# Two query chunks per slice of x, K before the second block of x, halved first slice and last sum, and a new instruction order, in a cross-attention kernel

## The chip, the core and the metric

The kernel runs on one core of one Trainium2 chip. The metric is device time in microseconds (us), the median of several executions. The core has a matrix engine (PE), a vector engine (DVE), an activation engine (ACT), a general engine (POOL), a queue engine that mostly issues transfers (SP), and 16 DMA engines that all transfers share.

## The reference

Two batches of 2048 tokens with 640 channels attend to 154 context rows of 1024 channels: 77 text rows and 77 image rows, each with its own softmax, 20 heads of 32 channels. Everything is float32.

```python
q = split_heads(x @ Wq.T)                       # (2, 20, 2048, 32)
k, v       = text @ Wk.T,  text @ Wv.T          # context rows 0..76
k_ip, v_ip = ip @ Wk_ip.T, ip @ Wv_ip.T         # context rows 77..153
out = softmax(q k^T / sqrt(32)) v + softmax(q k_ip^T / sqrt(32)) v_ip
return merge_heads(out) @ Wo.T + bo + x
```

## The kernel before, in words

Channels lie on the partitions. A batch is cut into blocks of 512 tokens (`xs`, four tiles of 128 x 5 x 512); one channel chunk `c` holds four heads (128 channels), so there are 5 chunks in each of 2 batches, 10 in all, and each has two halves of 1024 tokens: 20 units `u` (`step_of`, L116). A unit of batch 0 has its queries from two blocks of x, `(u, 0)` and `(u, 1)`; unit 0 is chunk 0 of blocks 0 and 1, unit 1 is chunk 0 of blocks 2 and 3, unit 2 is chunk 1 of blocks 0 and 1, unit 4 is chunk 2 of blocks 0 and 1.

Nothing is scheduled automatically. The order of the program is a list of some 900 words, `SCHEDULE` (L560), which `emit` (L630) turns into instructions one after the other; each engine carries out its own in that order. The letters that matter here:

- `q.u.h@bank`: the queries of a unit from one block, 5 matmuls of 128x512 (`queries`, L196-199; weights in `wqs`, three tiles used in turn); `cq.u.h`: ACT scales them into a tile `qT` (L207-209).
- `k.c.t`, `v.c.t`: the key or value projection of chunk `c`, for text or image rows, 8 matmuls (L136-140), with weights that `LK.n` loads (`load_w`, L126-130) into one of four slots; `ck`, `cv`: ACT copies the result (L684, L686).
- `R<s>.u@half`: the scores of a third of a unit, on a four-way row-tiled array into four of the eight PSUM banks (L224-231). `K`: ACT copies the four banks to `pb` (L239-243). `M`: DVE takes the row maxima (L275-282). `S`: POOL subtracts them (L291-293). `E`: ACT takes exponentials (L297-299, one instruction, or one per 77 scores with the maximum as its bias, L259-267, for the thirds in the sets `DIRECT` and `BIASED`; `DIRECT` reads the scores in PSUM and has no `K` and no `S`, `BIASED` has no `S`; `SUMMED` takes the row sums along). `D`, `I`, `N`, `T`: row sums and reciprocals on DVE, scaling on POOL (L312-314), a transpose on DVE (L318-321).
- `A.q@half`: probabilities times values for a chunk, 160 small matmuls into four banks (L323-330); `CA.q`: ACT empties those four banks (L347-357).
- `o`, `p`, `m`, `G`, `W`, `z`: the output projection of batch 0 by a fast scheme with 7 products, between the units of batch 1; `V`, `X`, `F`, `Y`: that of batch 1 by a longer scheme, in which `F` is one product (L839-846) and `Y` adds it to a sum on DVE (`add_part`, L786-796) and, with the last part, stores the sum from SP.
- `LX`, `LQ`, `LO`, `SF`, `SS`, `VS`: transfers, all issued from SP. Eight transfers may be under way; each waits for the one eight places earlier in its list.

The opening (L522-557) stands ahead of `SCHEDULE`. It issues block 0 of x in five slices and chunk 0 of Wq in five pieces, by turns from SP and ACT, then from SP block 1 of x, Wq chunk 1, half of the context, the first K weight, the other half, the second K weight, blocks 2 and 3 of x, and the V weights. PE makes 7 small matmuls on zeros, then three query chunks, `(0,0)`, `(0,1)` and `(2,0)`, each after the other, and then the two K projections of chunk 0. The first scores `R0.0` open `SCHEDULE`.

Of the kernel before, what the change touches and what calls it, by code (L numbers as in the profile page):

```python
# [9 lines left out]
F32 = mybir.dt.float32  # L10
# [4 lines left out]
B, S, C, CC, LT = 2, 2048, 640, 1024, 154  # L15
# [5 lines left out]
def kernel(  # L21
# [43 lines left out]
        (11, 0), (12, 0), (13, 0), (13, 2), (15, 1), (15, 2), (16, 2), (18, 1), (19, 2),  # L65
    }
    BIASED = {
        (3, 2), (4, 2), (6, 2), (8, 2), (9, 2), (11, 2), (12, 1), (14, 0), (18, 2),
    }
    SUMMED = {  # L70
        (4, 2), (11, 2), (12, 0), (13, 0), (13, 2), (14, 0), (15, 1), (15, 2), (18, 1), (18, 2), (19, 2),
# [3 lines left out]
    OPEN = 4  # L75
    HT = TB // 2

# [7 lines left out]
    wqs = [const.tile([P, NC, P], F32, name=f"wq_{n}") for n in range(3)]  # L85
# [5 lines left out]

    acc = const.tile([P, NC - 1, TB], F32, name="acc")
# [103 lines left out]
    def queries(u, h, pq):  # L196
        q = step_of(u)[0]
        for k in range(NC):
            nc.tensor.matmul(  # L199
                pq,  # L200
                wqs[q % 3][:, k, :],
                xs[place_of(u, h)][:, k, :],
                start=(k == 0),
                stop=(k == NC - 1),
            )

    def take_queries(u, h, pq):  # L207
        qT = qpool.tile([P, TB], F32, tag="qT", name=f"qT_{u}_{h}")
        nc.scalar.mul(qT, pq, SCALE)  # L209
        qTs[(u, h)] = qT  # L210
# [313 lines left out]
    for k in range(NC):  # L524
        load_x(queues[k % 2])
        queues[1 - k % 2].dma_start(out=wqs[0][:, k, :], in_=WqT[ts(k, P), :P])  # L526
    for _ in range(NC):
        load_x()
    load_wq(1)
# [11 lines left out]
    load_wq(2)  # L541
# [6 lines left out]
    FIRST = ((0, 0), (0, 1), (2, 0))  # L548
    for n, (u, h) in enumerate(FIRST):
        queries(u, h, banks[G + n])  # L550
        take_queries(u, h, banks[G + n])
    for t in range(2):
# [71 lines left out]
    ).split()  # L624

    late = [tuple(int(x) for x in w.split(".")[1:]) for w in SCHEDULE if w[:2] == "LX"]
    JOINS = {3: 5, 6: 1, 7: 6, 4: 7}
    at = {}

# [259 lines left out]
```

## Time and profile before

| what | us |
|---|---|
| median of 3 runs (lowest, highest) | 496.85 (496.82, 496.97) |
| the profiled execution, its own time | 497.84 |
| its span on the core | 496.0 |
| PE busy in the span | 489.1 |
| DVE busy | 413.0 |
| POOL busy | 370.3 |
| ACT busy | 301.4 |

Device time is a little more than the span, which runs from the first to the last record on the core. Views used later: a table by stage (busy time of each engine between two moments, with the number of instructions that start there, the mean granted TensorE clock, the share of the DMA engines and GB/s), the instructions in order of time (start, busy, engine, line, operation, tiles, shapes and count, and in brackets the idle time before with what ended it), and the chain that ended last, in order of time (start, length, what). A float32 matmul leaves two records, so `x10` is five matmuls. SPq and ACTq are the queues of SP and ACT at the issue of transfers; PEld is the load of weights.

### The profile page before, as it was taken

To read this page: it belongs to the slowest core of one execution; us is meant where nothing else is said; L and a number is where in the kernel's file an instruction comes from. 1 tells how busy PE (TensorE), PEld (TensorE's weight loads), DVE (VectorE), ACT (ScalarE), POOL (GpSimd) and SP (SyncE) were. 2 spreads that over 40 slices of the span, in tenths; PEclk is the share of its full clock that TensorE was granted. 3 is DMA by queue.
4 is the path that set the end of the run, shared out by engine and by line. 5 is a ranking of instruction groups with operands and counts; after the bars stand their busy time and mean duration, and the time that the engine had idled before them with its cause. 6 is when DMAs were issued, how large, how long until landed. Compare 5 with 4: busy or idle time off the path is not lost.

```text
span 496.0 us, 10378 instructions
## 1 busy us (share of the span) xinstructions
PE 489.1 (99%) x4114; PEld 288.5 (58%) x4114; DVE 413.0 (83%) x417; ACT 301.4 (61%) x929; POOL 370.3 (75%) x158
## 2 busy tenths in 40 slices
PE   8999999999999999999999999999999999999997
PEld 4676657467467556456556654754755675444442
DVE  0069999979999989979979796777999888999885
ACT  1175858977687778677999869677666962100000
POOL 0069998889988989788977798365989989249820
PEclk9999999999999999999999999999999999999999
DMA  8994404142425435395671359344551221510125
GB/s 267 351 260 128 120 3 130 49 112 74 109 65 170 125 120 165 119 380 204 194 236 49 113 159 316 133 127 140 166 174 45 62 91 42 171 63 23 43 85 211
DMA packets 67472, 69.38 MB, mean 140 GB/s; under 512 B 5472, under 2 KB 47200, under 8 KB 67424
## 3 DMA queue, kind: packets, MB, share of 16 engines
q1 hardware_dynamic: 66704, 68.00, 43.6%
q8 instruction: 32, 0.52, 0.5%
q10 hardware_dynamic: 720, 0.72, 0.5%
q14 instruction: 16, 0.13, 0.1%
HBM read 54.94 MB, written 10.49 MB: 132 GB/s over the span
## 4 chain that ended last, share of the span: by engine, by line
PE 95%; DMA 3%; SPq 1%; ACTq 0%; ACT 0%; DVE 0%; issue 0%
PE bank L199 33%; PE bank L846 11%; PE bank L330 11%; PE bank L231 11%; PE bank L488 10%; PE bank L140 9%; PE bank L469 7%; PE bank L498 3%; DMA aT<-in_L_xattn_Wk_ip_dram 2%; DMA x<-in_x_dram 1%; SPq L532 1%; ACTq L526 0%; SPq L130 0%; DVE acc L792 0%; ACT pb L243 0%
## 5 line engine op out<-in xcount | busy, mean ns | idle before, releaser
L314 POOL TENSOR_TENSOR pb<-pb,rden 128x1848 f32<-128x1848 f32 (+1 forms) x60 | 175.9, 2943 | 25.6 <-DVE rden L309 25.0
L199 PE MATMUL bank<-x,wq 128*128 128x512 f32 x400 | 179.6, 598 | 1.5 <-DMA x<-in_x_dram 1.4
L293 POOL TENSOR_TENSOR pb<-pb,mx 128x1848 f32<-128x1848 f32 (+1 forms) x42 | 128.2, 3066 | 58.5 <-DVE mx L279 58.3
L199 PEld LDWEIGHTS bank<-x,wq 128*128 128x128 f32 x400 | 73.5, 190 | 87.4 <-issue 81.6
L321 DVE STREAM_TRANSPOSE pb<-pb 128x1920 f32<-128x1920 f32 (+1 forms) x60 | 115.5, 1935 | 6.7 <-POOL pb L314 6.7
L279 DVE TENSOR_REDUCE mx<-pb 128x24 f32<-128x1848 f32 (+1 forms) x51 | 93.8, 1850 | 32.0 <-ACT pb L243 31.8
L243 ACT COPY pb<-bank 128x462 f32<-128x462 f32 (+1 forms) x204 | 87.1, 537 | 34.6 <-PE bank L231 34.0
L304 DVE TENSOR_REDUCE den<-pb 128x24 f32<-128x1848 f32 (+1 forms) x49 | 91.5, 1875 | 18.6 <-ACT pb L299 15.8
L299 ACT ACTIVATE pb<-pb 128x1848 f32<-128x1848 f32 (+1 forms) x42 | 69.3, 1651 | 18.6 <-POOL pb L293 18.5
L231 PEld LDWEIGHTS bank<-kT,qT 32*128 32x128 f32 x1280 | 45.5, 184 | 26.3 <-issue 16.6
L267 ACT ACTIVATE pb<-bank,mx 128x77 f32<-128x77 f32 x184 | 53.1, 380 | 10.8 <-DVE mx L282 10.8
L231 PE MATMUL bank<-kT,qT 32*128 32x154 f32 x1280 | 56.6, 306 | 0.3 <-ACT kT L557 0.3
L330 PE MATMUL bank<-pb,v 32*32 32x512 f32 x1600 | 55.2, 597 | 0.0
L267 ACT ACTIVATE pb<-pb,mx 128x77 f32<-128x77 f32 x160 | 47.3, 373 | 0.0
L140 PE MATMUL bank<-wo_ct,aT 128*128 128x154 f32 x320 | 45.8, 297 | 0.4 <-DMA aT<-in_L_xattn_Wk_ip_dram 0.4
L140 PEld LDWEIGHTS bank<-wo_ct,aT 128*128 128x128 f32 x320 | 42.8, 188 | 3.4 <-issue 2.2
L330 PEld LDWEIGHTS bank<-pb,v 32*32 32x32 f32 x1600 | 30.6, 103 | 21.6 <-issue 9.2
L209 ACT ACTIVATE qT<-bank 128x512 f32<-128x512 f32 x40 | 24.2, 614 | 27.4 <-PE bank L199 27.4
L267 ACT ACTIVATION_READ_ACCUMULATOR pb<-bank,mx 128x1 f32 x144 | 36.7, 258 | 0.0
L469 PE MATMUL bank<-aT,wo_ct 128*128 128x512 f32 x80 | 36.4, 595 | 0.0
L488 PE MATMUL bank<-aT,wo_ct 128*128 128x256 f32 x128 | 32.0, 384 | 0.0
L488 PEld LDWEIGHTS bank<-aT,wo_ct 128*128 128x128 f32 x128 | 23.8, 190 | 7.7 <-issue 4.5
(76 smaller groups left out, 427.9 us busy)
## 6 DMA issues: line engine op xcount, KB each, us to landing
x<-in_x_dram SPq DMA_DIRECT2D x20, 1280.0 KB, 7.3
out_dram<-acc SPq DMA_DIRECT2D x20, 256.0 KB, 2.6
x<-in_x_dram SPq DMA_DIRECT2D x18, 256.0 KB, 5.4
acc<-in_x_dram SPq DMA_DIRECT2D x16, 256.0 KB, 3.4
out_dram<-x SPq DMA_DIRECT2D x15, 256.0 KB, 2.0
v<-vS SPq DMA_DIRECT2D x160, 20.0 KB, 2.1
wq<-in_L_xattn_Wq_dram SPq DMA_DIRECT2D x9, 320.0 KB, 4.7
aT<-in_L_xattn_Wk_dram SPq DMA_DIRECT2D x5, 512.0 KB, 5.5
```

The costliest lines, as they stand in the source:

```text
L140: nc.tensor.matmul(keys_in(out), loaded[n][:, k, :], cT[:, k, :, t, :], start=(k == 0), stop=(k == NCC - 1))
L199: nc.tensor.matmul(pq, wqs[q % 3][:, k, :], xs[place_of(u, h)][:, k, :], start=(k == 0), stop=(k == NC - 1),)
L231: nc.tensor.matmul(ps[g][:, ts(t, 2 * L)], qTs[(u, h)][g * D : (g + 1) * D, ts(st, P)], kT[g * D : (g + 1) * D, c, b].rearrange("p t l -> ...
L243: nc.scalar.copy(keys_of(u, s)[:, :, g], ps[g][:, : n * 2 * L].rearrange("p (n l) -> p n l", n=n))
L267: nc.scalar.activation(row, row if ps is None else rows_in(ps[g], n)[:, t, x], AF.Exp, bias=maxs[(u, s)][:, *one], accum_out=None if den i ...
L279: nc.vector.tensor_reduce(mx, rows_of(u, s), AX.X, ALU.max, negate=negate)
L293: nc.gpsimd.tensor_tensor(rows_of(u, s), rows_of(u, s), maxs[(u, s)].unsqueeze(3).to_broadcast([P, n, 2, L]), ALU.subtract)
L304: nc.vector.tensor_reduce(den_of(u, s), rows_of(u, s), AX.X, ALU.add)
L314: nc.gpsimd.tensor_tensor(rows_of(u, s), rows_of(u, s), rdens[(u, s)].unsqueeze(3).to_broadcast([P, n, 2, L]), ALU.mult)
L321: nc.vector.transpose(p, p)
L330: nc.tensor.matmul(pa[r][g * D : (g + 1) * D, :], v4s[q % 2][rows, g, k, :], zones[rows, :, g, k, :], start=(k == 0), stop=(k == NK - 1),)
L488: nc.tensor.matmul(part, w_of[m][:, kp, op], t_of(m, b, i)[:, kp], start=(op == kp == 0 and m in (1, 2, 5)), stop=(op == 1 and kp == 1 and ...
```

## The change

- The opening gets chunks 0 and 1 of Wq together. Block 0 of x is loaded as before but its first slice comes in two halves of 256 tokens, from SP and ACT. PE makes chunks `(0,0)` and `(2,0)` side by side, both from each slice of x as it comes, the first slice in halves; then `(4,0)`, with Wq chunk 2, from the same block of x. `(0,1)` becomes the first word of `SCHEDULE`.
- SP's list after block 0: Wq chunk 2, context, first K weight, context, second K weight, then block 1 of x, block 2, the V weights, block 3.
- The queries `(2,0)` and `(4,0)` are kept in two tiles of `aT` that are free until chunk 3, not in `qpool`.
- The last `F` and the last `Y` of `SCHEDULE` are made in two halves of 256 columns, and the last sum is stored in two halves, one from SP and one from ACT.
- `DIRECT`, `BIASED` and `SUMMED` change for some thirds: in batch 0, `(3,2)` goes from biased to direct, and `(2,0)` and `(5,2)` become biased. In all ACT has 424 single-row exponentials in place of 344, 38 whole ones in place of 42, and 200 copies `K` in place of 204; POOL has 98 subtractions and scalings in place of 102.
- `SCHEDULE` is new from its first word to its last; the words are nearly the same.

```diff
     DIRECT = {
-        (11, 0), (12, 0), (13, 0), (13, 2), (15, 1), (15, 2), (16, 2), (18, 1), (19, 2),
+        (3, 2), (11, 0), (12, 0), (13, 0), (13, 2), (15, 0), (15, 1), (16, 2), (18, 1), (19, 2),
...
     BIASED = {
-        (3, 2), (4, 2), (6, 2), (8, 2), (9, 2), (11, 2), (12, 1), (14, 0), (18, 2),
+        (2, 0), (4, 2), (5, 2), (6, 2), (8, 2), (9, 2), (11, 2), (12, 1), (14, 1), (15, 2), (17, 2), (18,
+        2),
...
+    EARLY = (2, 0), (4, 0)
+    SIDES = slice(0, HT), slice(HT, TB)
...
+    q_early = aT[:, ds((NC - 1) * NHB, 2), :]
...
     queues = nc.sync, nc.scalar
-    for k in range(NC):
+    slices.pop(0)
+    for n, cols in enumerate(SIDES):
+        queues[n].dma_start(out=xs[0][:, 0, cols], in_=xT[:P, cols])
+        queues[1 - n].dma_start(out=wqs[n][:, 0, :], in_=WqT[:P, ts(n, P)])
+    for k in range(1, NC):
         load_x(queues[k % 2])
-        queues[1 - k % 2].dma_start(out=wqs[0][:, k, :], in_=WqT[ts(k, P), :P])
-    for _ in range(NC):
-        load_x()
-    load_wq(1)
+        queues[1 - k % 2].dma_start(
+            out=wq_all[:, :2, k, :], in_=WqT[ts(k, P), : 2 * P].rearrange("p (c o) -> p c o", c=2)
+        )
+    load_wq(2)
...
     load_w(2)
     load_w(3)
-    load_wq(2)
+    for _ in range(NC):
+        load_x()
...
-    FIRST = ((0, 0), (0, 1), (2, 0))
-    for n, (u, h) in enumerate(FIRST):
-        queries(u, h, banks[G + n])
-        take_queries(u, h, banks[G + n])
+    first = [(2 * c, 0, banks[G + c]) for c in range(3)]
+    for n, cols in enumerate(SIDES):
+        for c, (_, _, pq) in enumerate(first[:2]):
+            nc.tensor.matmul(
+                pq[:, cols], wqs[c][:, 0, :], xs[0][:, 0, cols], start=(n == 0), stop=False, skip_group_check=True
+            )
+    for k in range(1, NC):
+        for u, h, pq in first[:2]:
+            queries(u, h, pq, (k,), loose=True)
+    queries(*first[2])
+    for u, h, pq in first:
+        take_queries(u, h, pq)
...
     SCHEDULE = (
-        "R0.0@0 R1.0@1 K0.0 q.1.0@0 LK.5 SF.0.0 K1.0 M0.0 LK.4 M1.0 S0.0 R2.0@1 cq.1.0 v.0.0@1 K2.0 S1.0 M2.0 E0.0 "
...
-        "T1.1 S0.2 q.4.0@3 K1.2 T2.1 cq.3.1 S2.2 M1.2 E0.2 A.0@1 D0.2 S1.2 E2.2 cq.4.0 D2.2 I0.2 E1.2 N0.2 R0.3@0 "
-        "CA.0 D1.2 v.1.1@4 K0.3 I1.2 T0.2 N1.2 k.2.1@7 LK.11 cv.1.1 M0.3 R2.3@0 LK.13 ck.2.1 R1.3@1 LK.10 K2.3 T1.2 "
...
+        "q.0.1@4 R0.0@0 cq.0.1 LK.4 R1.0@1 K0.0 q.1.0@0 LK.5 K1.0 M0.0 M1.0 S0.0 R2.0@1 q.1.1@1 K2.0 S1.0 M2.0 E0.0 "
...
+        "cq.3.0 T2.0 R0.2@0 K2.2 k.2.1@5 I1.1 K0.2 I2.1 M2.2 N1.1 T0.1 R1.2@0 LK.8 LQ.3 v.1.0@6 K1.2 LK.13 M0.2 "
+        "N2.1 q.3.1@4 LK.10 T1.1 E0.2 S2.2 T2.1 M1.2 A.0@0 LQ.4 S1.2 cv.1.0 E2.2 D0.2 cq.3.1 ck.2.1 D2.2 E1.2 "
+        "R0.3@1 I0.2 I2.2 N0.2 CA.0 D1.2 v.1.1@0 K0.3 I1.2 N2.2 T0.2 cv.1.1 R1.3@1 R2.3@0 M0.3 N1.2 K1.3 k.2.0@4 "
...
-            nc.vector.tensor_tensor(t, t, ps, op)
+            for cols in sides:
+                nc.vector.tensor_tensor(t[:, cols], t[:, cols], ps[:, cols], op)
...
-            nc.sync.dma_start(out=outT[ts(m, P), ds(S + i * TB, TB)], in_=t)
+            for queue, cols in zip(queues, sides):
+                tokens = ds(S + i * TB + cols.start, cols.stop - cols.start)
+                queue.dma_start(out=outT[ts(m, P), tokens], in_=t[:, cols])
```

More of the change, by code (lines that the diff above doesn't have):

```diff
@@ L64 @@
     DIRECT = {
-        (11, 0), (12, 0), (13, 0), (13, 2), (15, 1), (15, 2), (16, 2), (18, 1), (19, 2),
+        (3, 2), (11, 0), (12, 0), (13, 0), (13, 2), (15, 0), (15, 1), (16, 2), (18, 1), (19, 2),
     }
     BIASED = {
-        (3, 2), (4, 2), (6, 2), (8, 2), (9, 2), (11, 2), (12, 1), (14, 0), (18, 2),
+        (2, 0), (4, 2), (5, 2), (6, 2), (8, 2), (9, 2), (11, 2), (12, 1), (14, 1), (15, 2), (17, 2), (18,
+        2),
     }
     SUMMED = {
-        (4, 2), (11, 2), (12, 0), (13, 0), (13, 2), (14, 0), (15, 1), (15, 2), (18, 1), (18, 2), (19, 2),
+        (3, 2), (4, 2), (11, 2), (12, 0), (13, 0), (13, 2), (14, 1), (15, 0), (15, 1), (17, 2), (18, 1),
+        (18, 2), (19, 2),
     }
@@ L74 @@
     NU = NP * SUB
-    OPEN = 4
+    EARLY = (2, 0), (4, 0)
     HT = TB // 2
+    SIDES = slice(0, HT), slice(HT, TB)
     const = ctx.enter_context(tc.tile_pool(name="const", bufs=1))
@@ L84 @@
     halves = banks[:G], banks[G:]
-    wqs = [const.tile([P, NC, P], F32, name=f"wq_{n}") for n in range(3)]
+    wq_all = const.tile([P, 3, NC, P], F32, name="wq_all")
+    wqs = [wq_all[:, n] for n in range(3)]
     bo_sb = const.tile([P, NC], F32, name="bo_sb")
@@ L194, with queries @@
     qTs = {}
-    def queries(u, h, pq):
+    def queries(u, h, pq, ks=range(NC), loose=False):
         q = step_of(u)[0]
-        for k in range(NC):
+        for k in ks:
             nc.tensor.matmul(
@@ L204, in queries @@
                 stop=(k == NC - 1),
+                skip_group_check=loose,
             )
     def take_queries(u, h, pq):
-        qT = qpool.tile([P, TB], F32, tag="qT", name=f"qT_{u}_{h}")
+        if (u, h) in EARLY:
+            qT = q_early[:, EARLY.index((u, h))]
+        else:
+            qT = qpool.tile([P, TB], F32, tag="qT", name=f"qT_{u}_{h}")
         nc.scalar.mul(qT, pq, SCALE)
@@ L523 @@
     queues = nc.sync, nc.scalar
-    for k in range(NC):
+    slices.pop(0)
[3 more added lines that the diff above has]
+    for k in range(1, NC):
         load_x(queues[k % 2])
-        queues[1 - k % 2].dma_start(out=wqs[0][:, k, :], in_=WqT[ts(k, P), :P])
-    for _ in range(NC):
-        load_x()
-    load_wq(1)
+        queues[1 - k % 2].dma_start(
+            out=wq_all[:, :2, k, :], in_=WqT[ts(k, P), : 2 * P].rearrange("p (c o) -> p c o", c=2)
+        )
+    load_wq(2)
     half = NCC // 2
@@ L560 @@
     SCHEDULE = (
[63 rows of a table removed]
[63 rows of a table added]
     ).split()
+    CLOSING = {[w for w in SCHEDULE if w[0] == kind][-1].partition("@")[0] for kind in "FY"}
     late = [tuple(int(x) for x in w.split(".")[1:]) for w in SCHEDULE if w[:2] == "LX"]
@@ L784, in sum_at, with sides_of, add_part @@
         return acc[:, m] if m < NC - 1 else res
-    def add_part(o, ps, op):
+    def sides_of(name):
+        return SIDES if name in CLOSING else (slice(0, TB),)
+    def add_part(o, ps, op, sides=(slice(0, TB),)):
         t = sum_at(o)
@@ L845, in finish @@
             w, x = PRODUCTS[m].split()
-            nc.tensor.matmul(
-                at[(c, h)], weight(w), tokens_of(x)[:, h], start=first, stop=True, skip_group_check=True
-            )
+            for cols in sides_of(".".join((k, *args))):
+                nc.tensor.matmul(
+                    at[(c, h)][:, cols],
+                    weight(w),
+                    tokens_of(x)[:, h][:, cols],
+                    start=first,
+                    stop=True,
+                    skip_group_check=True,
+                )
         elif k[0] == "Y":
             c, h, t = int(k[1:]), int(args[0]), args[1]
-            add_part((int(t[0]), NH * int(t[1]) + h), at[(c, h)], sign_of[(c, t)])
+            sides = sides_of(".".join((k, *args)))
+            add_part((int(t[0]), NH * int(t[1]) + h), at[(c, h)], sign_of[(c, t)], sides)
         else:
```

119 rows, old and new, of the table SCHEDULE are left out of this document.

## The prediction, made before the run

> **What bounds the kernel now.** I read the page first, then a table by stage, then the chain that ended last.
>
> ```profile
> PE 489.1 (99%) x4114; PEld 288.5 (58%) x4114; DVE 413.0 (83%) x417; ACT 301.4 (61%) x929; POOL 370.3 (75%) x158
> ```
> ```profile
> core 0: us, PE busy (x) PEld busy (x) DVE busy (x) ACT busy (x) POOL busy (x), PEclk, DMA share, GB/s
> 0.00:4.36 4.36, 3.31 (x15) 3.07 (x15) 0.17 (x1) 0.00 (x0) 0.83 (x6) 1.00 0.55 166
> 4.36:24.42 20.06, 17.97 (x64) 9.86 (x63) 0.00 (x0) 3.70 (x8) 0.00 (x0) 1.00 1.03 339
> 24.42:492.30 467.88, 467.79 (x4038) 275.52 (x4038) 412.12 (x415) 297.70 (x922) 369.46 (x152) 1.00 0.42 131
> 492.30:496.00 3.70, 0.01 (x1) 0.00 (x0) 0.69 (x1) 0.00 (x0) 0.00 (x0) 0.98 0.40 148
> ```
>
> From the first scores (24.42) to 492.30 PE is busy 467.79 of 467.88 us: there PE's own work is the time. Before 24.42 it is idle 20.06 - 17.97 = 2.09 us after its first real matmul, with the DMA engines full (share 1.03). So a gain needs less PE work, an earlier end of the opening, or a shorter tail, and it lasts only if PE is not made to wait afterwards. The chain names the opening's transfers:
>
> ```profile
> 2.14 6.40 DMA x<-in_x_dram
> 12.94 8.75 DMA aT<-in_L_xattn_Wk_ip_dram
> ```
> ```profile
> 4.36 2.84 PE L199 MATMUL bank<-x,wq 128*128 128x512 f32 x6
> 8.58 10.57 PE L199 MATMUL bank<-x,wq 128*128 128x512 f32 x24 [1.38 <-DMA x<-in_x_dram]
> 18.98 2.35 PE L140 MATMUL bank<-wo_ct,aT 128*128 128x154 f32 x16
> 21.73 2.37 PE L140 MATMUL bank<-wo_ct,aT 128*128 128x154 f32 x16 [0.40 <-DMA aT<-in_L_xattn_Wk_ip_dram]
> 24.42 1.85 PE L231 MATMUL bank<-kT,qT 32*128 32x154 f32 x48 [0.31 <-ACT kT L557]
> ```
>
> The last slice of x lands at 2.14 + 6.40 = 8.54, the second K weight at 12.94 + 8.75 = 21.69. Its projection starts 21.73, and the scores 0.31 after its end, when ACT has copied the keys.
>
> **Change, part 1: the opening.** Ahead of the second K weight, x block 1 goes away (five slices, 5 x 256 KB = 1.311 MB) and Wq chunk 2 takes the place of chunk 1, which itself now comes with block 0: 320 KB (0.328 MB) more in all.
>
> ```profile
> x<-in_x_dram SPq DMA_DIRECT2D x18, 256.0 KB, 5.4
> wq<-in_L_xattn_Wq_dram SPq DMA_DIRECT2D x9, 320.0 KB, 4.7
> ```
> ```profile
> 12.00:16.00 4.00, 4.00 (x11) 1.73 (x10) 0.00 (x0) 0.60 (x1) 0.00 (x0) 1.00 1.06 325
> 20.00:24.00 4.00, 3.60 (x26) 3.23 (x24) 0.00 (x0) 0.35 (x2) 0.00 (x0) 1.00 1.05 384
> ```
>
> At the rate seen for x slices with large neighbours (384 GB/s) block 1 is 3.41 us; at the rate seen with Wq pieces (325) the chunk is 1.01 us. So the second K weight lands 2.4 us earlier, at 19.3. At 325 for both it would be 3.0 earlier, at 384 for both 2.6; I keep 2.4, the smallest.
>
> By the Trainium skill ("DMA: Bandwidth & Descriptors", Specifications) a core gets about 358 GB/s of HBM; block 1 would then be an estimated 3.66 us and the sum 0.25 us lower. The 384 GB/s above is over that figure, so the measurement decides.
>
> PE is ready then. Its last piece of block 0 comes later by the 320 KB, about 1 to 1.6 us: 9.6 to 10.1. Behind it stand 14 records (four of two chunks, ten of chunk `(4,0)`) at 4.29/10 = 0.43 us (rows below): 6.0, end 16.1 at most. K1 takes 2.35, to 18.5, so PE waits some 0.8 for the second weight. K2 runs 19.3 to 21.65. The key copy's wait now lies under `q.0.1` (4.29), and the scores start at 25.95. Before, PE had at 24.42 made one query chunk less; the same point was 24.42 + 4.29 = 28.71. **PE is ahead by 2.8 us**: 2.4 by bytes, 0.4 by waits covered.
>
> But the first scores come 25.95 - 24.42 = **1.5 us later**, and with them the chain of the softmax, which starts there:
>
> ```profile
> 27.42 4.06 DVE L279 TENSOR_REDUCE mx<-pb 128x24 f32<-128x1848 f32 x2 [26.42 <-ACT pb L243]
> 29.58 3.29 POOL L293 TENSOR_TENSOR pb<-pb,mx 128x1848 f32<-128x1848 f32 x1 [28.22 <-DVE mx L279]
> ```
> ```profile
> 42.00:48.00 6.00, 6.00 (x26) 3.83 (x26) 6.00 (x5) 2.89 (x7) 6.00 (x3) 1.00 0.55 149
> 60.00:66.00 6.00, 6.00 (x36) 2.84 (x35) 6.00 (x4) 2.68 (x7) 6.00 (x3) 1.00 0.28 89
> 66.00:72.00 6.00, 6.00 (x88) 2.82 (x98) 6.00 (x5) 5.11 (x7) 6.00 (x3) 1.00 0.00 0
> 72.00:78.00 6.00, 6.00 (x136) 4.43 (x121) 4.30 (x5) 4.66 (x8) 4.91 (x3) 1.00 0.03 5
> ```
>
> DVE and POOL are full in these stages (6.00 of 6.00): a chain that starts 1.5 us late stays late until about 72, where the first gaps are.
>
> **Part 2: where PE meets that chain.** PE's first close meeting with it is at the end of the first attend:
>
> ```profile
> 64.56 8.74 POOL L293 TENSOR_TENSOR pb<-pb,mx 128x1848 f32<-128x1848 f32 x3
> 67.88 2.04 DVE L279 TENSOR_REDUCE mx<-pb 128x24 f32<-128x1848 f32 x1
> 73.34 1.75 ACT L299 ACTIVATE pb<-pb 128x1848 f32<-128x1848 f32 x1 [1.53 <-POOL pb L293]
> 74.99 2.03 ACT L353 COPY aT<-bank 128x512 f32<-128x512 f32 x4
> 76.11 4.48 PE L140 MATMUL bank<-wo_ct,aT 128*128 128x154 f32 x32
> 76.89 1.92 ACT L243 COPY pb<-bank 128x462 f32<-128x462 f32 x4
> 80.52 1.20 PE L231 MATMUL bank<-kT,qT 32*128 32x154 f32 x28
> ```
>
> In both orders `v.1.1` uses the first bank that `CA.0` empties, and `CA.0` stands on ACT behind `E1.2`, which waits for POOL's subtraction (end 64.56 + 8.74 = 73.30). One of four copies (2.03/4 = 0.5) frees the bank at 75.5; PE came at 76.11, with 0.6 to spare. After: chain 1.5 later, bank free at 77.1 (rounded up by 0.1). The new order removes one subtraction in front (`S0.2`, 3.29 on POOL), but DVE's maximum `M1.2` (end 69.92) stands beside it, on an engine without a gap, so 1.5 remains. PE comes at 76.11 - 2.8 + 2.2 (`k.2.1`, half of the 4.48, is now made earlier) + 0.2 = 75.8. **Wait 1.3.** Behind it PE makes `v.1.1` (2.2), to 79.3, then `R1.3` in the banks that `K0.3` empties: before 76.89 + 1.92 = 78.81, now 80.3. **Wait about 0.9.** A third meeting lies near 93, where `R2.4` and `R0.4` need exponentials that hang on POOL. I take 0.3, from a lead of 0.6 that is left; bounds 0 and 0.9. Sum 2.5. If no wait came back the sum would be 0; if every slack were gone, 2.8 + 1.5 = 4.3.
>
> **Part 3: switches of the array.** A query chunk next to row-tiled scores is longer:
>
> ```profile
> 44.29 4.29 PE bank L199 x10
> 59.75 4.49 PE bank L199 x10
> ```
>
> So 0.2 us at a change between whole-array and tiled matmuls. The built order after makes 108 such changes, before 106: two more, +0.4 (bounds 0 and 0.8, as the 0.2 may fall on one side or on both).
>
> **Part 4: conversions.** ACT gets 80 single-row exponentials more, loses 4 whole ones and 4 copies; POOL loses 4 operations.
>
> ```profile
> 86.58 4.08 ACT L267 ACTIVATE pb<-pb,mx 128x77 f32<-128x77 f32 x16
> L299 ACT ACTIVATE pb<-pb 128x1848 f32<-128x1848 f32 (+1 forms) x42 | 69.3, 1651 | 18.6 <-POOL pb L293 18.5
> ACT pb L243 <- PE bank L231: 34.0, 23, 4.4
> ```
>
> A row costs 4.08/16 = 0.25, a third of 24 rows 6.1 against 1.65: 4.4 us more on ACT each time. In all 80 x 0.25 - 4 x 1.65 = 13.4 us on an engine with 301.4 of 496 busy; ACT's waits for scores alone are 34.0. I cost it at nothing; the cover is that slack, and where it lacks, see rival C. Seven sums of V weights go from DVE to POOL and two others back: both engines have gaps there, nothing.
>
> **Part 5: the tail.**
>
> ```profile
> 491.29 1.02 PE L846 MATMUL bank<-pb,wo_ct 128*128 128x512 f32 x2
> 492.35 0.69 DVE L792 TENSOR_TENSOR acc<-acc,bank 128x512 f32<-128x512 f32 x1 [1.03 <-PE bank L846]
> 493.07 0.33 SPq L796 DMA_DIRECT2D out_dram<-acc  x1
> ```
>
> Two halves of the last product are the same columns. If the first half of the sum runs beside the second product, the end moves up by about half of 0.69; against it, two DVE instructions have two starts. I take 0, bounds -0.3 and +0.3. The store's landing (496.0) follows an issue of the same kind; the queue of ACT is empty then.
>
> Moved at no cost: SP's list (x block 1 lands by 22.7, five slices of 0.68 behind the second K weight; slice k is needed by `q.0.1` at 21.65 + 0.86 k), the two early query tiles, the store pieces.
>
> **Sum**, against the own time 497.84 (span 496.0 and 1.84 around it): -2.8 + 2.5 + 0.4 + 0 = +0.1, so 497.9. The median of the runs is 0.99 lower than that one execution, so 496.85 + 0.1, **497.0**.
>
> **Rivals.**
> A, the forecast: the lead goes back as waits at 76 to 94. 497.0.
> B, faster: the chain catches up before 76 because `(2,0)` no longer needs its subtraction and POOL was what held `S1.2` (it is full in 60 to 72). Then waits are 0 to 1.5 rather than 2.5: 496.85 - 2.4 + 0 to 1.5 = 494.4 to 495.9. For it: POOL full; against: DVE full too.
> C, slower: ACT becomes the bound. At each converted third PE must wait for what stands behind 4.4 us more of ACT. It decides where ACT's slack is under 4.4, as in 66 to 72 (busy 5.11 of 6.00). At six such places with 0.45 each: +2.7, 499.6. Against: ACT's 61%.
> D, the change doesn't do what it says: the second K weight lands hardly earlier, because more pieces wait for a free place in the issue list and the DMA engines run dry. Only the 0.4 of covered waits is won, the first scores are at 28.3, the chain 3.9 late, and the waits, worked as in part 2, are 1.3 and 1.1 at the two banks and 0.5 at the third: 496.85 - 0.4 + 2.9 + 0.4 = 499.75. It decides if the weight lands after 20.5. Against: a DMA share over 1.0 from 4.36 on.
> E, the clock: the opening's PE gaps lower the granted clock. Here a gap of 1.38 before 8.58 left PEclk at 1.00; one window of eight records at half speed would add 8 x 0.43/2 = 1.7: 498.7. The Trainium skill ("TensorE: Matmul & The Clock Gate", Part 1: The HAM clock gate) says that about 3.4 us of idleness halve the clock; no gap here would be so long.
>
> **How the numbers follow.** A 0.44, B 0.28, C 0.17, D 0.09, E 0.02. About 0.2% (1.0 us, 495.86 to 497.84) is what a measurement of this kernel can tell from no change; so same 0.44, faster 0.28, slower 0.28. A's own range is 495.9 to 497.8 (third wait 0 to 0.9, changes 0 to 0.8, tail 0.3 either way, not all at one end at once). The range, 495.0 to 499.2, holds A, half of B, and most of C: 0.44 + 0.14 + 0.13, with E and a little of D about 0.8.
>
> **What would show it.** Right: second K projection at 19.3 (0.8 of wait before it), first scores near 26, first DVE maximum near 29; PE waits on ACT of about 1.3 and 0.9 near 76 and 79, little behind 95; PE busy up by 0.4. B shows no PE wait at 76 to 94. C shows PE waits behind L308, or L276, at several places after 100. D shows the second K projection after 20.5. E shows PEclk under 1.00 in the first 30 us. I am wrong in the main if PE's waits behind the first scores sum to less than 1.0 or more than 4.

## The result, and the profile after

| what | before | changed |
|---|---|---|
| median, us (11 runs each, same chip) | 497.0 | 498.38 |
| lowest to highest | 496.82 to 498.04 | 497.94 to 498.52 |
| the profiled execution, its own time | 497.84 | 498.45 |
| its span | 496.0 | 496.7 |

The ratio is 1.0022, with a 95% interval of 1.0013 to 1.0031: slower by about 1.1 us. The forecast was 497.0 with a range of 495.0 to 499.2. So the time lies in the range, and the change is no gain. The prediction took 0.2% for the least difference that can be told; whether the loss is just under or just over that, the interval leaves open. The execution of before that was profiled was one of its longer ones, so the spans differ by 0.7 only.

The first line of the page of the changed kernel, and PE's start in order of time:

```profile
PE 490.7 (99%) x4120; PEld 291.3 (59%) x4120; DVE 412.5 (83%) x414; ACT 314.8 (63%) x1041; POOL 360.4 (73%) x159
```
```profile
4.20 3.02 PE L565 MATMUL bank<-x,wq_all 128*128 128x256 f32 x8
7.42 11.40 PE L204 MATMUL bank<-x,wq_all 128*128 128x512 f32 x26 [0.21 <-DMA wq_all<-in_L_xattn_Wq_dram]
18.66 4.38 PE L145 MATMUL bank<-wo_ct,aT 128*128 128x154 f32 x32
22.87 4.45 PE L204 MATMUL bank<-x,wq_all 128*128 128x512 f32 x10
27.25 1.85 PE L240 MATMUL bank<-kT,qT 32*128 32x154 f32 x48
```

From 7.42 to the first scores PE has no gap. Both K projections stand in one row of 32 records: the second no longer waits for its weight. This is the issue of that weight on SP (start, length), and from the view of transfers its us to landing in the last column:

```profile
10.63 1.24 SPq L135 DMA_DIRECT2D aT<-in_L_xattn_Wk_ip_dram  x1
```
```profile
aT<-in_L_xattn_Wk_ip_dram SPq DMA_DIRECT2D x1, 512.0 KB, 7.9
```

It lands at 10.63 + 7.9 = 18.5, 3.2 us earlier than before, while PE comes to it only at about 20.8, with the 17th of the 32 records. So from 7.42 on the new opening is bound by PE's own work, no longer by bytes. The first scores are at 27.25 against 24.42: **2.8 us later**. PE has by then made one query chunk more, so it is 28.71 - 27.25 = **1.46 us ahead**.

Where that lead goes, first at `v.1.1` (instructions of several engines in order of time):

```profile
70.26 2.03 DVE L288 TENSOR_REDUCE mx<-pb 128x24 f32<-128x1848 f32 x1
...
72.37 3.29 POOL L302 TENSOR_TENSOR pb<-pb,mx 128x1848 f32<-128x1848 f32 x1 [2.63 <-DVE mx L288]
...
75.70 1.75 ACT L308 ACTIVATE pb<-pb 128x1848 f32<-128x1848 f32 x1 [0.75 <-POOL pb L302]
...
77.35 2.03 ACT L362 COPY aT<-bank 128x512 f32<-128x512 f32 x4
...
77.97 2.38 PE L145 MATMUL bank<-wo_ct,aT 128*128 128x154 f32 x16 [0.67 <-ACT aT L362]
```

Read it upwards: PE waits for the first copy of `CA.0`, that for `E1.2`, that for the subtraction on POOL, and POOL has idled 2.63 for DVE's maximum. DVE sets the chain. POOL's subtraction ends at 75.66, against 73.30 before: of the 2.83 the chain was late, 0.47 is made up. Then the scores `R1.3` and `R2.3`, in the changed kernel and in the one before:

```profile
80.27 2.52 PE L240 MATMUL bank<-kT,qT 32*128 32x154 f32 x40
82.72 2.38 PE L145 MATMUL bank<-wo_ct,aT 128*128 128x154 f32 x16
...
94.04 0.81 PE L240 MATMUL bank<-kT,qT 32*128 32x154 f32 x16 [0.36 <-ACT kT L707]
```
```profile
80.52 1.59 PE L231 MATMUL bank<-kT,qT 32*128 32x154 f32 x40
82.04 2.38 PE L140 MATMUL bank<-wo_ct,aT 128*128 128x154 f32 x16
```

The same 40 records take 82.72 - 80.27 = 2.45 from start to next start, and took 1.52: 0.93 of waiting that carries no bracket, since it lies inside a row (the modelled ends hide it). The third wait, 0.36, is at 94.04, for a copy of keys that stands on ACT behind `E1.3`. By stage, changed kernel:

```profile
60.00:80.00 20.00, 19.33 (x289) 13.68 (x284) 18.42 (x15) 17.39 (x47) 16.23 (x6) 1.00 0.48 121
80.00:100.00 20.00, 19.64 (x130) 11.32 (x129) 19.13 (x19) 17.93 (x66) 17.77 (x8) 1.00 0.08 21
100.00:492.00 392.00, 391.82 (x3363) 228.28 (x3362) 346.00 (x357) 252.89 (x884) 298.17 (x132) 1.00 0.43 136
```

After 100 PE is full again. Its second attend starts at 107.64 against 106.76, the attends behind it are 0.72 to 0.87 later than before, and the last product is 0.88 later. The end:

```profile
492.17 1.03 PE L876 MATMUL bank<-pb,wo_ct 128*128 128x256 f32 x4
493.23 0.75 DVE L819 TENSOR_TENSOR acc<-acc,bank 128x256 f32<-128x256 f32 x2 [0.31 <-PE bank L876]
...
494.02 0.35 ACTq L825 DMA_DIRECT2D out_dram<-acc  x1
```

From the last product's start to the end of the span it is 496.7 - 492.17 = 4.5, and was 496.0 - 491.29 = 4.7.

### The profile page after: what moved, and what is told of

Its sections match the earlier page's. It is cut to its first block, busy times and chain, and to the rows that moved or that the text cites. A ratio compares the mean times of both kernels' runs of the same rounds, so it can differ in the third digit from the quotient of the medians.

```text
span 496.7 us, 10533 instructions
## 1 busy us (share of the span) xinstructions
PE 490.7 (99%) x4120; PEld 291.3 (59%) x4120; DVE 412.5 (83%) x414; ACT 314.8 (63%) x1041; POOL 360.4 (73%) x159
## 4 chain that ended last, share of the span: by engine, by line
PE 84%; DVE 7%; POOL 4%; ACT 2%; DMA 1%; issue 0%; SPq 0%; DVEq 0%; POOLq 0%
PE bank L204 29%; PE bank L876 11%; PE bank L497 10%; PE bank L339 10%; PE bank L240 9%; PE bank L478 7%; PE bank L145 5%; POOL pb L302 3%; PE bank L507 3%; DVE mx L288 3%; DVE pb L330 2%; DVE den L313 2%; DMA wq_all<-in_L_xattn_Wq_dram 1%; POOL pb L323 1%; ACT pb L308 1%; ACT pb L252 0%
## 5 line engine op out<-in xcount | busy, mean ns | idle before, releaser
L204 PE MATMUL bank<-x,wq_all 128*128 128x512 f32 x396 | 177.4, 598 | 0.3 <-DMA wq_all<-in_L_xattn_Wq_dram 0.2
L302 POOL TENSOR_TENSOR pb<-pb,mx 128x1848 f32<-128x1848 f32 (+1 forms) x38 | 117.3, 3097 | 59.1 <-DVE mx L288 57.7
L204 PEld LDWEIGHTS bank<-x,wq_all 128*128 128x128 f32 x396 | 73.0, 190 | 85.1 <-issue 81.9
L288 DVE TENSOR_REDUCE mx<-pb 128x24 f32<-128x1848 f32 (+1 forms) x50 | 91.8, 1847 | 35.2 <-ACT pb L252 35.0
L313 DVE TENSOR_REDUCE den<-pb 128x24 f32<-128x1848 f32 (+1 forms) x47 | 87.8, 1879 | 14.9 <-ACT pb L308 10.8
L308 ACT ACTIVATE pb<-pb 128x1848 f32<-128x1848 f32 (+1 forms) x38 | 63.3, 1669 | 18.2 <-POOL pb L302 18.1
L276 ACT ACTIVATE pb<-bank,mx 128x77 f32<-128x77 f32 x208 | 60.5, 395 | 5.7 <-DVE mx L291 5.7
L276 ACT ACTIVATE pb<-pb,mx 128x77 f32<-128x77 f32 x216 | 63.2, 380 | 1.4 <-DVE mx L288 1.4
L240 PE MATMUL bank<-kT,qT 32*128 32x154 f32 x1216 | 54.8, 305 | 0.4 <-ACT kT L707 0.4
L276 ACT ACTIVATION_READ_ACCUMULATOR pb<-bank,mx 128x1 f32 x168 | 44.5, 278 | 0.0
```

The lines of the kernel that those rows point to most:

```text
L204: nc.tensor.matmul(pq, wqs[q % 3][:, k, :], xs[place_of(u, h)][:, k, :], start=(k == 0), stop=(k == NC - 1), skip_group_check=loose,)
L240: nc.tensor.matmul(ps[g][:, ts(t, 2 * L)], qTs[(u, h)][g * D : (g + 1) * D, ts(st, P)], kT[g * D : (g + 1) * D, c, b].rearrange("p t l -> ...
L276: nc.scalar.activation(row, row if ps is None else rows_in(ps[g], n)[:, t, x], AF.Exp, bias=maxs[(u, s)][:, *one], accum_out=None if den i ...
L288: nc.vector.tensor_reduce(mx, rows_of(u, s), AX.X, ALU.max, negate=negate)
L302: nc.gpsimd.tensor_tensor(rows_of(u, s), rows_of(u, s), maxs[(u, s)].unsqueeze(3).to_broadcast([P, n, 2, L]), ALU.subtract)
L313: nc.vector.tensor_reduce(den_of(u, s), rows_of(u, s), AX.X, ALU.add)
```

## The experiments

Theory: the new opening starts the vector chain 2.8 us late, and that chain, not one bank or one engine, takes PE's lead back before 114. Rivals: the new order of the list costs; ACT's extra exponentials cost; bytes still set the first scores. Each run is compared with runs of the kernel before on its own chip.

**e1: the new opening in front of the old order.**

```diff
     SCHEDULE = (
-        "q.0.1@4 R0.0@0 cq.0.1 LK.4 R1.0@1 ... (the new list)
+        "q.0.1@4 R0.0@0 cq.0.1 R1.0@1 K0.0 q.1.0@0 ... (the list of before, without q.4.0 and cq.4.0)
```

(and the choice of exponentials of before)

> The new opening in front of the old instruction order and the old choice of exponentials (only the query chunk (0,1) is put ahead of the first scores and the chunk (4,0) is left out of the list, since the opening now makes it). Theory (the vector chain starts 2.8 us later and takes PE's lead back, whatever the order): first scores at 27.2 as in the changed kernel; PE comes to v.1.1 at 76.11 - 1.46 = 74.65 and its bank comes free at 75.5 + 2.84 = 78.3, so a wait of about 3.7; PE then goes on with the chain's delay, and the time is 2.0 to 2.8 over the kernel before, 499.0 to 499.8. Rival (the opening is good by its 1.46, the new order spoils it): no new waits, 1.0 to 1.5 under the kernel before, 495.5 to 496.0.

Measured: 500.44, ratio 1.0066 (1.0051 to 1.0081). PE's wait comes earlier than I thought, at the first attend, and then the stage in which it lies:

```profile
70.58 7.16 PE L337 MATMUL bank<-pb,v 32*32 32x512 f32 x160 [2.82 <-ACT qT L216]
```
```profile
70.00:74.00 4.00, 3.42 (x69) 2.31 (x74) 4.00 (x3) 3.15 (x3) 4.00 (x3) 0.64 0.02 4
```

The opening alone loses 3.3 us. The wait is 2.82, and behind it the attend takes 7.16 in place of 5.52, at a granted clock of 0.64: that is why the loss is above my 2.0 to 2.8. The theory holds in sign and kind; its place was off.

**e2: the old opening in front of the new order.**

```diff
-        "q.0.1@4 R0.0@0 cq.0.1 LK.4 R1.0@1 ...
+        "R0.0@0 LK.4 R1.0@1 ...
-        "N2.1 q.3.1@4 LK.10 ... cq.3.1 ck.2.1 ...
+        "N2.1 q.3.1@4 q.4.0@7 LK.10 ... cq.3.1 cq.4.0 ck.2.1 ...
```

(and the opening's transfers and query chunks as before)

> The old opening (transfers and the three query chunks as before) in front of the new order and the new choice of exponentials; (0,1) leaves the list and (4,0) is put back in it behind q.3.1. Theory: first scores at 24.4, no waits of PE at v.1.1, at R1.3 and near 94; what is left is one more visit to the scores, +0.4 to +0.5: 497.3 to 497.6, under the changed kernel by 0.7 to 1.1. Rival (the opening's lead is real and is kept): 1.5 over the changed kernel, 499.8. Rival (the new order itself costs, by ACT's extra exponentials): as the changed kernel or slower, with PE waits after 100.

Measured: 497.35, ratio 0.9998 (0.9987 to 1.0009). PE's first scores, and two stages:

```profile
23.50 1.85 PE L240 MATMUL bank<-kT,qT 32*128 32x154 f32 x48 [0.31 <-ACT kT L566]
```
```profile
60.00:80.00 20.00, 20.00 (x252) 12.37 (x245) 16.84 (x12) 15.72 (x42) 16.22 (x7) 1.00 0.46 115
80.00:100.00 20.00, 20.00 (x137) 12.15 (x136) 19.03 (x18) 18.26 (x71) 15.92 (x6) 1.00 0.15 41
```

The same list and the same exponentials, with the scores at 23.5: no wait with a bracket is left behind them, and the time cannot be told from that of before. (The row of 40 scores near 80 takes 1.81 from start to next start, against 1.52 before, so 0.29 of waiting may be left inside it.) The interval lies wholly under that of the changed kernel. So the opening costs, and not the order or ACT's exponentials in the main. A little may be theirs: from the first scores to the second attend PE takes 83.09 us here and 82.34 in the kernel before, 0.75 more, which the times do not show.

**e3: two slices of block 1 of x ahead of the K weights.**

```diff
+    load_x()
+    load_x()
     load_wq(2)
     half = NCC // 2
```

> The changed kernel with two of the five slices of block 1 of x (512 KB) put ahead of Wq chunk 2 and so ahead of the context and both K weights. Theory (PE's own work bounds the new opening from the landing of the second slices at 7.3 on; the second K weight lands 2.3 us before PE comes to it): the weights land about 1.4 later, first scores stay at 27.2 within 0.1, time within 0.3 of the changed kernel. Rival, the prediction's step (bytes ahead of the second K weight set the first scores): first scores 1.4 later, 28.6, and the time 0.7 to 1.4 over the changed kernel.

Measured: 497.83, ratio 1.0013 (1.0004 to 1.0022). PE, then the issue of the second K weight and its us to landing:

```profile
17.51 4.38 PE L145 MATMUL bank<-wo_ct,aT 128*128 128x154 f32 x32
21.73 4.45 PE L204 MATMUL bank<-x,wq_all 128*128 128x512 f32 x10
26.11 1.85 PE L240 MATMUL bank<-kT,qT 32*128 32x154 f32 x48
```
```profile
11.22 0.94 SPq L135 DMA_DIRECT2D aT<-in_L_xattn_Wk_ip_dram  x1
```
```profile
aT<-in_L_xattn_Wk_ip_dram SPq DMA_DIRECT2D x1, 512.0 KB, 7.7
```

512 KB more ahead of the weight, and it lands at 11.22 + 7.7 = 18.9, 0.4 later and not 1.4 as I expected; PE comes to it at 19.62. The scores are not 1.4 later but 1.1 earlier: the bytes ahead of the second K weight do not set them, against the prediction's step. The edit does not explain that they are earlier, as it stands behind the second slices in the list. The second slices landed sooner in this execution, as the trace's landing times of the pieces (16 for a transfer) show:

```text
second piece of Wq, changed kernel: 14 of 16 landed by 6.05, the last two at 7.15 and 7.29
second piece of Wq, e3:             15 of 16 landed by 5.55, the last at 6.05
```

The 11 runs of e3 fall in two groups, five at 497.26 to 497.47 and five at 498.21 to 498.45 (one between), and the higher group is the changed kernel's range. The profiled execution (497.31) is of the lower group. I take it, without proof, that a late piece divides them. In nine profiled executions with the halved first slice the second piece of Wq had landed by 6.97 to 7.47 in eight, and by 6.05 only here; why it came early here is open.

How much an early opening is worth can be read from the start of the second attend, in the changed kernel and in e3:

```profile
107.64 5.52 PE L339 MATMUL bank<-pb,v 32*32 32x512 f32 x160
```
```profile
106.50 5.52 PE L339 MATMUL bank<-pb,v 32*32 32x512 f32 x160
```

From the first scores to there PE takes 80.39 us in both (27.25 to 107.64, 26.11 to 106.50), and also in e4 (27.14 to 107.53) and in e10 (26.18 to 106.57). So with this list the waits behind the first scores are the same whenever the scores come, and an opening that is 1.1 us shorter is 1.1 us gained: the spans of e3 and e10 are 495.5 and 495.7, that of the changed kernel is 496.7. In e2, and in e6 below, the chunk `(4,0)` stands in this stretch and not ahead of the first scores; without its 4.29 they take 83.09 - 4.29 = 78.8. One query chunk more ahead of the first scores thus costs 1.6 us of waits, however early the scores are.

**e4: the last product and sum whole.**

```diff
-    CLOSING = {[w for w in SCHEDULE if w[0] == kind][-1].partition("@")[0] for kind in "FY"}
+    CLOSING = set()
```

> The changed kernel with the last product and the last sum whole again, one store from SP. Theory (halves give nothing: the second half of the sum still follows the end of the second product): within 0.3 of the changed kernel; the end after the last product's start, 4.7 us in the kernel before, the same within 0.2. Rival: the halves cost, 0.4 or more under the changed kernel; or they gain, 0.4 or more over it.

Measured: 498.4, ratio 1.0020 (1.0011 to 1.0029).

```profile
492.08 1.02 PE L876 MATMUL bank<-pb,wo_ct 128*128 128x512 f32 x2
...
493.13 0.69 DVE L819 TENSOR_TENSOR acc<-acc,bank 128x512 f32<-128x512 f32 x1 [0.31 <-PE bank L876]
```

From 492.08 to the span's end, 496.8, it is 4.7, with halves 4.5. The halves may give 0.2; the times do not tell it.

**e5: the first third's scores ahead of (0,1), (4,0) as filler.**

```diff
-    queries(*first[2])
-    for u, h, pq in first:
+    for u, h, pq in first[:2]:
         take_queries(u, h, pq)
     for t in range(2):
-
+        queries(*first[2], ((0,), (1, 2))[t], loose=True)
         ps = halves[t][G - 2 + t]
...
+    queries(*first[2], (3,), loose=True)
...
+        elif k == "H":
+            queries(*first[2], (4,), loose=True)
+            take_queries(*first[2])
...
-        "q.0.1@4 R0.0@0 cq.0.1 LK.4 R1.0@1 K0.0 q.1.0@0 ...
+        "R0.0@0 H K0.0 q.0.1@4 cq.0.1 LK.4 R1.0@1 q.1.0@0 ...
```

> The changed kernel with the same work in the opening in another order: the chunk (4,0) is cut up and fills the time until each K weight has landed (one matmul ahead of the first K projection, two between the projections, one behind the second, one behind the first scores), and the first third's scores R0.0 come ahead of the query chunk (0,1). Theory (the time lost is the late start of the vector chain): first scores at about 22.2 in place of 27.2, the third behind it at 28; the chain 2.0 to 2.4 earlier than in the changed kernel; PE's waits at v.1.1, at R1.3 and near 94 fall from 1.9 in all to under 0.6; two more changes of the array, +0.4; time 0.9 to 1.5 under the changed kernel, 496.9 to 497.5. Rival (the waits come from the new order of the list, not from the start): the same waits, and the time 0.4 over the changed kernel, 498.8.

Measured: 500.07, ratio 1.0060 (1.0047 to 1.0073). My expectation failed. PE and DVE of e5, then DVE of the changed kernel:

```profile
22.45 1.07 PE L240 MATMUL bank<-kT,qT 32*128 32x154 f32 x24
...
29.55 1.07 PE L240 MATMUL bank<-kT,qT 32*128 32x154 f32 x24 [0.69 <-ACT qT L218]
```
```profile
27.02 2.08 DVE L288 TENSOR_REDUCE mx<-pb 128x24 f32<-128x1848 f32 x1 [26.02 <-ACT pb L252]
32.55 2.08 DVE L288 TENSOR_REDUCE mx<-pb 128x24 f32<-128x1848 f32 x1 [3.46 <-ACT pb L252]
```
```profile
30.26 4.06 DVE L288 TENSOR_REDUCE mx<-pb 128x24 f32<-128x1848 f32 x2 [29.26 <-ACT pb L252]
```

One third was early, and DVE then idled 3.46 for the second. The second maximum ends at 34.63, in the changed kernel at 34.32: the chain as a whole started no earlier, and PE's waits at `v.1.1` and at 94 came back at the same size (0.7 and 0.4). PE itself lost time to two more changes of the array, 0.69 for the scaled queries, and 0.32 for the second half of the context, which I had forgotten. So "the first scores" was too narrow a cause; it is the time at which the chain can run without gaps.

**e6: (4,0) out of the opening.**

```diff
-    load_wq(2)
     half = NCC // 2
...
+    load_wq(2)
     nc.sync.dma_start(out=bo_sb, in_=bo.rearrange("(c p) -> p c", p=P))
...
-    queries(*first[2])
-    for u, h, pq in first:
+    for u, h, pq in first[:2]:
         take_queries(u, h, pq)
```

(and `q.4.0` in the list as in e2)

> The changed kernel with (4,0) out of the opening: its Wq chunk is loaded behind block 3 of x, and q.4.0 stands in the list behind q.3.1. Theory: the second K weight lands about 1.0 earlier, 17.5, PE has only two chunks ahead of K and comes to it at 16.5, so PE waits about 1.0; first scores at 24.0, as in the kernel before; no waits near 76 to 94; time as with the old opening, 497.0 to 497.5. Rival (the lead of the side-by-side opening is what counts): PE lost 1.0 more in the opening, the time 1.0 over the changed kernel.

Measured: 498.08, ratio 1.0014 (1.0004 to 1.0025).

```profile
17.36 2.38 PE L145 MATMUL bank<-wo_ct,aT 128*128 128x154 f32 x16 [0.45 <-DMA aT<-in_L_xattn_Wk_ip_dram]
...
23.95 1.85 PE L240 MATMUL bank<-kT,qT 32*128 32x154 f32 x48
```
```profile
60.00:80.00 20.00, 20.00 (x257) 12.41 (x258) 17.30 (x12) 15.26 (x41) 16.22 (x7) 1.00 0.45 116
```

The mechanism is as expected: scores at 23.95, no wait in 60 to 80. From the scores to the second attend it takes 83.10, like e2, and its scores are 0.45 later than those of e2. The time is 0.6 over the upper end of what I expected, and its interval overlaps that of the changed kernel: it does not separate the two.

**e7 and e9: the conversion of (2,0) undone.** In e7 `S0.2` was put right behind `M0.2`, in e9 ahead of `E0.2`.

```diff
-        (2, 0), (4, 2), (5, 2), (6, 2), ...
+        (4, 2), (5, 2), (6, 2), ...
-        ... M0.2 " "N2.1 q.3.1@4 LK.10 T1.1 E0.2 S2.2 ...
+        ... M0.2 S0.2 " "N2.1 q.3.1@4 LK.10 T1.1 E0.2 S2.2 ...   (e7)
+        ... M0.2 " "N2.1 q.3.1@4 LK.10 T1.1 S0.2 E0.2 S2.2 ...   (e9)
```

> The changed kernel with the third (2,0) exponentiated whole again, behind a subtraction on POOL (S0.2 put back ahead of E0.2), the conversion nearest to the waits undone. Theory (DVE is what holds S1.2 in the changed kernel, POOL idles 2.63 ahead of it; with 3.29 more on POOL, POOL holds it): S1.2 ends 0.6 later, PE's wait at v.1.1 is 1.3 in place of 0.7, time 0.3 to 0.8 over the changed kernel. Rival (the 4.4 us more of ACT work that the conversion brings are what PE waits for): the wait at v.1.1 falls, time 0.5 to 1.0 under the changed kernel.

Measured: 501.59, ratio 1.0088 (1.0074 to 1.0102). PE at the first attend, and the stage:

```profile
74.26 6.96 PE L339 MATMUL bank<-pb,v 32*32 32x512 f32 x160 [3.23 <-issue]
```
```profile
74.00:78.00 4.00, 3.74 (x76) 2.17 (x86) 4.00 (x3) 1.90 (x3) 2.62 (x2) 0.57 0.10 24
```

The place was a mistake: on POOL, `S0.2` came ahead of `N2.1`, which the attend needs. One operation of 3.29 us in the wrong place makes PE wait 3.23, and again the attend behind it is slow (granted clock 0.57). e9 puts it right:

> The third (2,0) exponentiated whole behind a subtraction on POOL as in the run before, but S0.2 stands on POOL behind N2.1, directly ahead of E0.2, so that it no longer holds up the transpose T2.1 and the first attend. Theory (DVE holds S1.2 in the changed kernel; with 3.29 more POOL holds it): wait at v.1.1 about 1.3 in place of 0.7, and since the ACT work that goes was idle cover, no gain elsewhere: 0.1 to 0.6 over the changed kernel. Rival (ACT's 4.4 us more are what PE waits for): under the changed kernel by 0.5 or more. If the run before was slow for the place of S0.2 alone, the 3.2 wait at A.0 is gone.

Measured: 498.5, ratio 1.0021 (1.0012 to 1.0031).

```profile
78.32 1.85 PE L145 MATMUL bank<-wo_ct,aT 128*128 128x154 f32 x12 [1.23 <-ACT aT L362]
```
```profile
67.27 8.74 POOL L302 TENSOR_TENSOR pb<-pb,mx 128x1848 f32<-128x1848 f32 x3
```

The wait at `v.1.1` is 1.23 in place of 0.67: with the third subtraction back, POOL works on without a gap to 76.01 and holds the chain, where in the changed kernel DVE held it. Behind the first scores PE has no other wait with a bracket in this run: the third, for a copy on ACT, is gone with the 4.4 us of ACT. From the first scores (27.03) to the second attend (107.79) PE takes 80.76, in the changed kernel 80.39. So the conversion helped by half a microsecond at one place, gave a part back at another, and is worth some 0.4 in the trace, which the times (498.5 and 498.38) do not tell. At `v.1.1` ACT's work is not what PE waits for.

**e8: a query chunk pulled ahead of the first attend.**

```diff
-        "N2.1 q.3.1@4 LK.10 ... cq.3.1 ck.2.1 ...
+        "N2.1 q.3.1@4 q.4.1@7 LK.10 ... cq.3.1 cq.4.1 ck.2.1 ...
-        "M2.3 E2.3 q.4.1@7 S0.3 ... T2.2 cq.4.1 SQ.1 VS.1.1 D0.3 E1.3 ck.2.0 I0.3 I2.3 "  "cq.5.0 R2.4@0 ...
+        "M2.3 E2.3 S0.3 ... T2.2 SQ.1 VS.1.1 D0.3 ck.2.0 cq.5.0 E1.3 I0.3 I2.3 "  "R2.4@0 ...
```

> The changed kernel with the query chunk (4,1) pulled ahead of the first attend A.0 (into bank 7, as (4,0) stood in the kernel before), so that PE comes to v.1.1 4.3 us later, and with the copies ck.2.0 and cq.5.0 put ahead of the exponential E1.3 on ACT. Theory (the whole vector chain is late up to about 114, not one bank): no wait at v.1.1 and R1.3, but the same 1.5 to 3 us come back at the next meetings, R2.4 and R0.4 at 91 to 96 and near 114; time within 1.0 of the changed kernel, 497.9 to 499.4. Rival (the place of v.1.1 behind CA.0 is all that costs): waits under 0.3 in all, 1.5 to 1.9 under the changed kernel, 496.5 to 496.9.

Measured: 499.76, ratio 1.0054 (1.0041 to 1.0066). PE's waits by what they were for (total us, times, longest):

```profile
PE bank L240 <- ACT kT L707: 1.3, 1, 1.3
PE bank L145 <- ACT aT L366: 1.1, 1, 1.1
...
PE bank L204 <- ACT pb L252: 0.8, 1, 0.8
```

The waits at 78 and 80 are gone (but for 0.29 inside the row at 83.74), and 1.3, 0.8 and 1.1 stand at 93.6, 96 and 115.7. The rival falls: filling this one hole did not keep the lead. It is 0.4 slower than the upper end that I expected. The second edit, which puts two copies ahead of `E1.3`, may be the reason; it was not tried apart.

**e10: the first slice of x whole.**

```diff
     slices.pop(0)
-    for n, cols in enumerate(SIDES):
-        queues[n].dma_start(out=xs[0][:, 0, cols], in_=xT[:P, cols])
-        queues[1 - n].dma_start(out=wqs[n][:, 0, :], in_=WqT[:P, ts(n, P)])
-    for k in range(1, NC):
+    slices.insert(0, (0, 0))
+    for k in range(NC):
         load_x(queues[k % 2])
```

(and the same in PE's first loop)

> The changed kernel with the first slice of x whole (one transfer, one piece of Wq for both chunks, whole matmuls). Theory (PE is bound from the landing of the second slices on, and these are issued 0.4 us earlier when two transfers go): first real matmul about 0.2 later, second slices land up to 0.4 earlier, first scores 0 to 0.4 earlier; time from 0.5 under the changed kernel to the same. Rival (the halves let PE start early and that counts): 0.3 or more over the changed kernel.

Measured: 498.22, ratio 1.0024 (1.0013 to 1.0036). In its profile the second slices landed by 5.65, the K projections started at 17.58 and the scores came at 26.18, with the same waits behind them. That execution (497.47) was the fastest of the eleven. By its times the kernel cannot be told from the changed one: the halves of the first slice are worth nothing that shows.

**e11: the kernel before once more.** No edit.

> The kernel before once more, for a second profile of its opening. If the last slice of x lands near 7.0 in place of 8.54, and the time is 0.8 or more under 497.84, then one late piece of one transfer, not the kernel, made the first profile's opening; if it lands at 8.5 again, the delay belongs to the kernel. Either way PE has no wait from the first scores to 492.

Measured: 497.82, one run.

```profile
21.68 2.37 PE L140 MATMUL bank<-wo_ct,aT 128*128 128x154 f32 x16 [0.31 <-DMA aT<-in_L_xattn_Wk_ip_dram]
24.37 1.85 PE L231 MATMUL bank<-kT,qT 32*128 32x154 f32 x48 [0.31 <-ACT kT L557]
```

The late slice of block 0, the one issued at 2.14 in the first profile, landed at 7.01 and not at 8.54, yet the time is the same, against my expectation: now a slice of block 1 had a late piece (15 of 16 by 8.74, the last at 9.78), and the second K weight was no earlier. A late piece moves from transfer to transfer; it does not belong to one. No version that I ran beats the kernel before beyond its interval.

## Why the prediction was right, and which terms were not

The sign of the mechanism held: PE gains a lead in the opening, the vector chain starts later, and the lead comes back as waits at the three places named. The sum came out near zero because both its large terms were too large, by 1.3 and 0.5; that they partly cancel is luck.

Of its signs, the waits near 76 and 79 came (0.67 and 0.93, smaller than said), and their sum with the third, 2.0, lies between the 1.0 and 4 that it named. The second K projection did not start at 19.3 with 0.8 of wait, but at 20.8 with none; the first scores came at 27.25 and not near 26, the first maximum at 30.26 and not near 29; and PE's busy time rose by 1.6, not 0.4, in part because the 0.93 inside a row counts as busy.


- **Opening, -2.8 forecast, -1.46 measured.** The step that failed is "Behind it stand 14 records ... 6.0, end 16.1 at most". It took for granted that PE would have the other 16 records done when the last piece landed. But PE can only start on the second slices when they land, at 7.29, and has 26 records from there: 26 x 0.429 = 11.2, end 18.66. Even with every slice in time, 30 records from 4.20 take 12.9, to 17.1, so 16.1 could not be met; the other 1.6 is the time lost until the second slices land, for which the sum has no term. Where they landed at 6.05 and 5.65 (e3, e10), the scores came at 26.11 and 26.18, close to the 25.95 forecast. The bytes were forecast well, even with care (19.3; 18.5 measured), but they bound nothing here: in e3 the weight landed 0.4 later and the scores no later. One reading was wrong without harm: the slice that landed at 8.54 is the fourth of block 0, not the last; six records, three slices, stand ahead of PE's wait for it.
- **First scores, 25.95 forecast, 27.25 measured**, so the chain is 2.8 late in place of 1.5: the same mistake.
- **Waits, 2.5 forecast, 2.0 measured**: 1.3, 0.9 and 0.3 against 0.67, 0.93 and 9.10 - 8.68 = 0.42 (the time from the two query chunks' start at 84.94 to the scores at 94.04, and before from 84.25 to 92.93). The chain was later than forecast by 1.3, but so was PE, and the removed `S0.2` let the chain catch up by 0.47, which the forecast had denied. (By its own terms, 75.8 should be 75.7, and the second wait 1.0.)
- **Changes of the array, +0.4 forecast, +0.38 measured**: the first attend starts at 70.78 - 69.66 = 1.12 later, with 2.20 of K projection made earlier, so 1.08 earlier net; of the 1.46, 0.38 is gone, as one more visit to the scores would cost.
- **Conversions, nothing forecast**: PE is busy 391.82 of 392 us after 100, the delay does not grow there (0.88, then 0.72 to 0.88), and the time of e2, with the same conversions, cannot be told from that of before. Rival C is refuted.
- **Tail, 0 forecast, -0.2 in the profiles**, within the bounds; not seen in the times.
- **Sum**: -1.46 + 0.38 + 2.0 - 0.2 = +0.7, the difference of the spans. The medians differ by 1.4, the ratio says 1.1: a part of the rest is that the profiled execution of before was a long one. In e2 the old opening ran without a late slice, and the scores came at 23.50. Against such an opening the lead is 23.50 + 4.29 - 27.25 = 0.54, and the sum would be an estimated -0.54 + 0.38 + 2.0 - 0.2 = +1.6; no execution of the kernel before with so early an opening was profiled.

Of the rivals, B was half right: POOL was relieved (2.63 idle ahead of `S1.2`), but DVE held the chain. D is refuted by the landing at 18.5; its sign, a second K projection after 20.5, did show, but because PE came late and not the weight. E did not occur in the changed kernel, but behind longer gaps the clock does fall: that added to the losses of e1 and e7. What decides is shown by e1 and e2 together: the new opening loses 3.3 us with the old order and 1.1 with the new one, and the new order with the old opening loses nothing that its times show.

What stays open: how to win back the 1.1. Second slices that land as in e3 and e10 are worth that much in the profiles, but the times of e6 and e10 are not told apart from the changed kernel's, and what makes single pieces of a transfer late was not found.

## What to carry to other kernels

When loads are cut so that an engine may start early, count the work that is still to do after each landing, not only after the last: the bound is the largest of the sums "landing plus what stands behind it". Work of the busiest engine that is put ahead of the chain that feeds its buffers is not all gained: here one query chunk ahead of the first scores cost 1.6 us of waits, however early the scores came. Ask for the engine and for the chain in the same unit of time, and look for the place where they next meet. A wait that is filled at one place in a late chain can appear at the next, as in e8.

## What the runs showed of the hardware

A gap on PE of 2.8 to 3.2 us costs more than itself. Behind 2.82 us of idleness (e1) the granted clock was 0.64 over the next stage, and the attend took 7.16 us in place of 5.52; behind 3.23 us (e7) 0.57, and 6.96 us. In both the granted clock is 0.50 for 3.4 us (71.14 to 74.56 in e1, 73.99 to 77.40 in e7). The gaps of 1.38 us in the kernel before and 1.34 us in e8 left the clock at 1.00. The Trainium skill ("TensorE: Matmul & The Clock Gate", Part 1: The HAM clock gate) puts the window of idleness that halves the clock at about 3.4 us; the runs agree in kind, and 2.82 us was already enough here.

The first matmuls of the changed kernel, of 256 columns, started 0.43 us apart five times, as far apart as those of 512 columns later, and then 0.22 apart. The table by stage gives a granted clock of 1.00 throughout, but the trace's own record of the clock begins only at 6.47, close to where the spacing changes. It is so in all nine profiled openings with such matmuls (the record begins at 5.05 in e3, where two were slow, and at 4.06 in e5, where none was). So the slow start is most likely a half clock that the table does not show. It cost nothing in the changed kernel, as the second slices were not there yet.

One or two of a transfer's 16 pieces landed 1 to 1.8 us after the others in several of the openings (6.05 and 7.29 in the changed kernel, 6.71 and 8.54 in the one before). That is as much as the whole change is worth, and it is the likely, but not shown, source of the scatter of about 1 us between runs of one kernel.
